# Routing tokens as two parts: one part's expert results scattered by token, the other's stored by tile and gathered at the end

## The chip, the cores and the metric

The kernel runs on one core of a Trainium2 chip, in one launch. The metric is the device time of that core in microseconds. Before the change it is 378.88 us, the median of 9 runs (375.48 to 384.29). The profile shows one execution of its own, which took 381.39 us; its span from the first to the last instruction is 379.7 us.

## The reference

Input x is 2 x 2048 tokens of 128 floats. Two blocks follow, each with a layer norm ahead of it and a residual around it:

```
x = x + attn(layernorm(x))    # a state-space layer: long convolution, gelu, a gated unit, a projection
x = x + ffn(layernorm(x))     # a mixture of experts
```

The second block is what matters here. Each of the 4096 tokens gets 14 gates (softmax of x @ router_w), keeps its top two and divides them by their sum. Expert e computes `silu(rmsnorm(x) * rms_w[e] @ w1[e]) @ w2[e]` with weights 128 x 256 and 256 x 128. The token's output is the gate-weighted sum of its two experts, plus two shared experts that every token passes through.

## The kernel before

Everything is float32. **The state-space layer** comes first and is left alone by the change.

**The routing stage** works on 32 chunks of 128 tokens, in five units u0 to u4 with chunks 0-3, 4-11, 12-19, 20-27 and 28-31 (class Unit, L657). A unit runs the gated unit and the output projection, adds to X, takes the layer-norm scales (`scales`, L720: some fourteen short VectorE operations), writes the normalised rows on ScalarE (`rows`, L735, into the tile `pl`), transposes them on TensorE, gets logits, picks two experts per token (`choose`, L777), counts tokens per expert (`count`) and turns counts into a slot number for each token and choice (`slots`, L826). `scatter` (L851) then issues two indirect DMAs per chunk on GpSimd (POOL). Each takes 128 rows of 130 floats (the row, its gate, and the number of the result row it belongs to) to their slots in the DRAM buffer `xs_rows`, where each expert has a region of its own. There are 64 such scatters.

**Shared experts** (class Shared, L946): eight blocks s0 to s7 of 512 tokens. Six of them stand in the hand-written list STEPS, between the units' steps; s6 and s7 come at the end (LATE = 2).

**The table** (`table`, L861): once all counts are known, about twenty short VectorE operations and a matmul give, for each tile of 128 slots, its expert and its first row.

**The tiles**: 77 tiles, a bound that holds for any counts. Per tile SP copies the expert's first weights into `wg` (L905, 12 tiles ahead), a DMA gathers 128 rows into `xg` (L911, 8 tiles ahead, on ScalarE's queue, the first even ones on SP's), TensorE transposes them (3 ahead), multiplies by `wg` (2 ahead), ScalarE applies silu (`hs`), and `outer` (L929) multiplies by the second weights, scales by the gate on VectorE (`yo`) and issues an indirect DMA on POOL that scatters 128 result rows by token into the DRAM buffer `res` (L940). Row numbers and experts are values in registers; every fourth tile ScalarE, SP and TensorE each load four of them (L1041). `xg` has 15 buffers and `yo` 10; the scatter reads its row numbers out of `xg`, so an `xg` buffer is free only when the scatter has landed.

**The end**: eight loads bring `res` back (L1003), s6 and s7 are computed, and VectorE adds the two results per token and X and stores (`finish`, L1006).

**Order.** From the routing stage on, VectorE, ScalarE and TensorE go through the wrapper Ordered (L643), which keeps their compute operations in the order in which they are written; the profile puts them all on L651. DMAs, register loads and everything on POOL are placed by the scheduler. Each engine then works through its own list from top to bottom, and a DMA issued from an engine's queue is an entry of that list.

Of the kernel before, what the change touches and what calls it, by code (L numbers as in the profile page):

```python
# [11 lines left out]
I32 = mybir.dt.int32  # L12
# [15 lines left out]
NTILE = (2 * NTOK + NE * (SLOTS - 1)) // SLOTS  # L28
ROW = P + 2
CAP = SLOTS + NTOK  # L30
# [19 lines left out]
u0.gate.0 u0.tanh.0 u0.value.0 u1.gate.0 u0.biased.0 u1.gate.1 u0.gated.0 u1.tanh.1  # L50
u1.value.1 u1.tanh.0 u0.project.0 u1.biased.1 u1.value.0 u0.add.0 u2.gate.1 u1.biased.0
u2.gate.0 u1.gated.1 u1.gated.0 u2.value.0 u2.tanh.0 u0.scales u1.project.0 u2.biased.0
u2.tanh.1 u1.project.1 u2.value.1 u1.add.0 u0.rows.0 u3.gate.0 u0.turn.0 u0.copies.0
u1.add.1 u0.turned.0 u2.biased.1 u0.logits.0 u1.scales u3.value.0 u2.gated.0 u1.rows.0
u0.unscale u2.project.0 u0.choose u1.rows.1 u1.turn.0 u1.copies.1 u2.add.0 u0.count u0.exps
u1.turned.0 u0.slots u1.turn.1 scale u1.logits.0 u1.turned.1 u1.copies.0 scale u1.logits.1
u1.unscale u0.scatter scale u2.gated.1 scale s0.first.0 scale u1.choose scale u2.project.1
s0.silu.0 scale u2.add.1 u1.count u1.exps s0.second.0 scale u1.slots scale scale u3.tanh.0
scale s0.first.1 scale u3.biased.0 u2.scales u1.scatter s0.silu.1 s0.second.1 u3.gated.0
u2.rows.0 s0.first.2 u2.rows.1 u2.turn.0 s0.first.3 s0.silu.2 u2.unscale s0.silu.3  # L60
s0.second.2 u2.turned.0 u2.turn.1 u2.logits.0 u2.turned.1 scale u2.logits.1 u2.copies.0
u3.project.0 u2.copies.1 u2.choose u3.gate.1 u4.gate.0 u3.tanh.1 u3.value.1 u4.tanh.0
u3.biased.1 u3.add.0 u2.count u4.value.0 u2.exps s0.second.3 u3.gated.1 u4.biased.0 u2.slots
s1.first.0 s1.first.1 s1.silu.0 u3.project.1 s1.silu.1 s1.second.0 u3.add.1 u2.scatter
s1.second.1 s1.first.2 s0.add u3.scales s1.silu.2 s1.second.2 u4.gated.0 u3.rows.0
s1.first.3 u3.rows.1 u3.turn.0 u4.project.0 u3.turned.0 u3.turn.1 u3.unscale u4.add.0
u3.turned.1 u3.logits.0 s1.silu.3 u3.logits.1 u3.copies.1 u3.copies.0 s1.second.3 u3.choose
s2.first.0 s2.silu.0 u3.count u3.exps s2.first.1 u3.slots s2.silu.1 s2.first.2 s2.first.3
u4.scales s2.second.0 u3.scatter s2.silu.3 s2.silu.2 s2.second.1 s1.add s2.second.2
u4.rows.0 s2.second.3 u4.copies.0 u4.turn.0 s2.add s3.first.0 u4.turned.0 u4.unscale  # L70
u4.logits.0 s3.silu.0 s3.first.1 u4.choose s3.silu.1 s3.second.0 s3.second.1 u4.exps
u4.count s3.first.2 u4.slots s3.silu.2 s3.first.3 s3.second.2 s3.silu.3 s3.second.3 s3.add
s4.first.0 s4.first.1 s4.silu.0 s4.first.2 s4.silu.1 s4.second.0 s4.silu.2 u4.scatter
s4.first.3 s4.second.1 s4.silu.3 scale s4.second.2 scale scale s4.second.3 s4.add s5.first.0
s5.first.1 s5.silu.0 s5.silu.1 s5.second.0 s5.second.1 s5.first.2 s5.silu.2 s5.first.3
s5.second.2 s5.silu.3 s5.second.3 s5.add
# [17 lines left out]
def s4d_glu_moe_kernel(  # L94
# [499 lines left out]
    pls = ctx.enter_context(tc.tile_pool(name="pls", bufs=3))  # L594
    xgp = ctx.enter_context(tc.tile_pool(name="xgp", bufs=15))
    yop = ctx.enter_context(tc.tile_pool(name="yop", bufs=10))
# [5 lines left out]

    xs_rows = nc.dram_tensor("xs_rows", (NE * CAP, ROW), F32).ap()
    xs_part = dram_disjoint_views(xs_rows, 2 * NT + 1)
    res = nc.dram_tensor("res", (2 * NTOK, P), F32).ap()
    res_part = dram_disjoint_views(res, NTILE)

# [467 lines left out]
    for _ in ends:  # L1077
        pass
# [49 lines left out]
```

## Time and profile before

| stage of the profiled execution | us from the span's start |
|---|---|
| state-space layer | 0 to 124 |
| routing up to the first scatter | 124 to 153.6 |
| scatters into xs_rows, 64 | 153.6 to 235.0 |
| table, first loads of weights and rows | 235 to 250 |
| 77 tiles on TensorE (first and last product `pz`) | 250.2 to 352.2 |
| last result scatter on POOL ends | 357.2 |
| loads of res, last sums, stores | 358.6 to 379.7 |

| engine | busy, us (share of the span) |
|---|---|
| TensorE (PE) | 270.7 (71%) |
| VectorE (DVE) | 231.3 (61%) |
| ScalarE (ACT) | 170.6 (45%) |
| GpSimd (POOL) | 148.6 (39%) |

The execution took 381.39 us, its span is 379.7 us, and the mean granted TensorE clock 0.873. The shares are averages over stages with different limits, so each stage is to be read by itself. In rows of the trace the first number is the start in us, the second the time in us, then engine, line, operation, what is written and read, and in brackets the engine's idle time before it and what ended that.

### The profile page before, as it was taken

To read this page: it belongs to the slowest core of one execution; us is meant where nothing else is said; L and a number is where in the kernel's file an instruction comes from. 1 tells how busy PE (TensorE), PEld (TensorE's weight loads), DVE (VectorE), ACT (ScalarE), POOL (GpSimd) and SP (SyncE) were. 2 spreads that over 40 slices of the span, in tenths; PEclk is the share of its full clock that TensorE was granted. 3 is DMA by queue.
4 is the path that set the end of the run, shared out by engine and by line. 5 is a ranking of instruction groups with operands and counts; after the bars stand their busy time and mean duration, and the time that the engine had idled before them with its cause. 6 is when DMAs were issued, how large, how long until landed. Compare 5 with 4: busy or idle time off the path is not lost.

```text
span 379.7 us, 8569 instructions
## 1 busy us (share of the span) xinstructions
PE 270.7 (71%) x2863; PEld 222.2 (59%) x2863; DVE 231.3 (61%) x718; ACT 170.6 (45%) x423; POOL 148.6 (39%) x230
## 2 busy tenths in 40 slices
PE   1900979748890997779798996087887778789940
PEld 1800659648790456546565774076787778779640
DVE  5789999999956298856857523133443444344074
ACT  3999869900233368967466542012322222323310
POOL 5300000000000200677777775036776776777400
PEclk9955599998995695789989699579999999999985
DMA  8100197953100790111111111267765656642098
GB/s 235 39 1 0 36 228 177 249 151 87 30 5 0 229 309 6 37 56 49 51 58 49 58 49 49 91 187 227 228 190 166 198 184 202 194 127 70 8 382 278
DMA packets 66894, 47.16 MB, mean 124 GB/s; under 512 B 7305, under 2 KB 64783, under 8 KB 66851
## 3 DMA queue, kind: packets, MB, share of 16 engines
q1 hardware_dynamic: 49714, 32.24, 28.6%
q0 software_dynamic: 4512, 8.47, 6.7%
q10 hardware_dynamic: 12624, 5.91, 6.1%
q8 instruction: 23, 0.38, 0.4%
q14 instruction: 21, 0.16, 0.1%
HBM read 24.49 MB, written 12.86 MB: 98 GB/s over the span
## 4 chain that ended last, share of the span: by engine, by line
DVE 39%; PE 31%; ACT 8%; issue 6%; DMA 5%; ACTq 5%; SPq 3%; POOL 1%; POOLq 0%; DVEq 0%
PE pz L651 11%; PE ph L651 8%; PE yps L558 4%; DVE t L329 3%; ACTq L1041 3%; DVE t L330 2%; ACTq L651 2%; PE pr L651 2%; DVE U L411 2%; ACT hs L651 2%; DMA xg<-xs_rows 2%; ACT junk L220 2%; DVE Y L568 2%; DVE sel L651 2%; ACT pl L651 2%
## 5 line engine op out<-in xcount | busy, mean ns | idle before, releaser
L940 POOL DMA_INDIRECT res<-yo,xg x77 | 75.7, 983 | 46.5 <-DMA xg<-xs_rows 17.0
L855 POOL DMA_INDIRECT xs_rows<-pl,si x64 | 62.0, 969 | 46.3 <-ACT WB L651 27.2
L651 ACT ACTIVATE hs<-ph 128x256 f32<-128x256 f32 x77 | 27.9, 382 | 90.4 <-PE ph L651 32.3
L651 DVE TENSOR_SCALAR yo<-pz,xg 128x128 f32<-128x128 f32 x77 | 27.0, 351 | 59.9 <-PE pz L651 57.6
L651 PE MATMUL pz<-WB,hs 128*128 x308 | 50.4, 286 | 17.0 <-ACT hs L651 16.6
L651 PEld LDWEIGHTS pz<-WB,hs 128*128 128x128 f32 x308 | 41.4, 193 | 21.6 <-ACT hs L651 20.5
L651 PE MATMUL ph<-xgt,wg 128*128 128x128 f32 x308 | 48.5, 281 | 0.2 <-DVE xgt L651 0.2
L651 PEld LDWEIGHTS ph<-xgt,wg 128*128 128x128 f32 x308 | 41.9, 197 | 0.6 <-DVE xgt L651 0.6
L613 POOL MEMSET blank<- 128x130 f32 x1 | 0.2, 207 | 97.5 <-DVE Y L568 97.5
L651 PEld LDWEIGHTS pz<-WB,hsh 128*128 128x128 f32 x192 | 25.5, 210 | 12.4 <-ACT hsh L651 9.5
L651 PE MATMUL pz<-WB,hsh 128*128 128x128 f32 x192 | 27.1, 298 | 4.9 <-ACT hsh L651 4.9
L651 DVE COPY xgt<-xgt 128x128 f32<-128x128 f32 x77 | 21.6, 282 | 10.9 <-PE xgt L651 10.8
L651 PE MATMUL xgt<-ident,xg 128*128 128x128 f32 x77 | 21.5, 282 | 9.1 <-DMA xg<-xs_rows 9.1
L651 PE MATMUL ph<-XRT,WB 128*128 128x512 f32 x48 | 27.8, 693 | 0.0
L651 ACT ACTIVATE hsh<-ph 128x512 f32<-128x512 f32 x24 | 14.0, 596 | 20.5 <-PE ph L651 20.5
L345 PE MATMUL kps<-PW,BC 128*8 128x128 f32 x128 | 6.5, 343 | 20.4 <-ACT junk L231 18.4
L472 PE MATMUL SP<-U,VT 128*32 128x32 f32 x512 | 14.2, 305 | 7.8 <-issue 5.3
L472 PEld LDWEIGHTS SP<-U,VT 128*32 128x32 f32 x512 | 13.5, 155 | 8.4 <-issue 5.7
L651 ACT ACTIVATE pl<-X,mr,rq_y 128x128 f32<-128x128 f32 x32 | 12.9, 482 | 12.0 <-DVE mr L651 12.0
L651 PE MATMUL pg<-Y,gluw 128*128 128x512 f32 x16 | 9.4, 706 | 10.8 <-DVE Y L568 10.8
L558 PE MATMUL yps<-PW,ST 32*32 32x128 f32 x512 | 15.2, 268 | 2.4 <-issue 1.6
L651 PEld LDWEIGHTS xgt<-ident,xg 128*128 128x128 f32 x77 | 11.1, 146 | 9.8 <-DMA xg<-xs_rows 9.8
(236 smaller groups left out, 549.9 us busy)
## 6 DMA issues: line engine op xcount, KB each, us to landing
wg<-WB SPq DMA_DIRECT2D x77, 128.0 KB
toep<-kp SPq DMA_DIRECT2D x24, 256.0 KB
xg<-xs_rows ACTq DMA_DIRECT2D x73, 65.0 KB
WB<-res SPq DMA_DIRECT2D x7, 512.0 KB
Y<-kp SPq DMA_DIRECT2D x8, 256.0 KB
WB<-in_w_dram SPq DMA_DIRECT2D x2, 896.0 KB
WB<-in_w_dram SPq DMA_DIRECT2D x4, 448.0 KB
out_dram<-WB SPq DMA_DIRECT2D x7, 256.0 KB
```

Of the source, the lines that this page charges most:

```text
L220: S.activation(junk, X[:, k, :], AF.Copy, accum_out=nm[:, k:k + 1])
L329: V.tensor_tensor(t1, low, bc(bc(Z[:, 0, k, qs], 1, 2), 3, m), ALU.mult)
L330: V.tensor_tensor(t2, low, bc(bc(Z[:, 1, k, qs], 1, 2), 3, m), ALU.mult)
L345: T.matmul(kps[a * NM:a * NM + 8, :], lhsT=BC[:, c, q, :], rhs=PW[:, c, q, 0:P], start=(i == 0 and c == 0), stop=False, skip_group_check=True,
L411: V.scalar_tensor_tensor(U[:, c, :], pu[:, k, :], rsr[:, c:c + 1], inb, ALU.mult, ALU.add)
L472: T.matmul(sp[j * NM:(j + 1) * NM, c, q - x * HQ, :], lhsT=VT[:, c, q, j * NM:(j + 1) * NM], rhs=U[:, :, 4 * q + j], start=True, stop=True,)
L558: T.matmul(ysum[g][js, u, :], lhsT=ST[js, c, q, :], rhs=PW[js, c, q, 1:P + 1], start=False, stop=(c == 1), skip_group_check=True,)
L568: V.transpose(Y.rearrange("p k t -> p t k"), YC)
L651: return tc.keep_in_program_order(getattr(self.engine, name)(*args, **kwargs))
L855: G.indirect_dma_start(out=xs_part[2 * (k0 + k) + a], out_offset=bass.IndirectOffsetOnAxis(ap=si[:, a, k:k + 1], axis=0), in_=pl[:, a, k, ...
L940: G.indirect_dma_start(out=res_part[t], out_offset=bass.IndirectOffsetOnAxis(ap=xg[:, P + 1:P + 2].bitcast(I32), axis=0), in_=yo, in_offse ...
L1041: return nc.values_load_multi_w_load_instructions(where[0:1, i, t:min(t + GRP, NTILE)], engines=engines, min_val=0, max_val=most, skip_run ...
```

## The change

Tokens go in two parts, chunks 0-19 (u0, u1, u2) and chunks 20-31 (u3, u4), each with an `xs_rows`, a count and a table of its own. Part 0 has 53 tiles and part 1 has 37, 90 in all. Part 0's results are scattered by token into `res` as before. Part 1's are stored tile by tile into a new DRAM buffer `ys` by a plain DMA on SP's queue, and at the end 24 indirect DMAs on POOL (`picked`, L1044 of the changed kernel) gather each token's two rows from `ys`. The tile loop runs over part 0 and then part 1.

STEPS is a new order. Shared experts s0 to s3 stand in it, and s4 to s7 come at the end. `table.0` follows `u2.slots`, and `table.1` follows `u4.slots`. The source emits u4's eight scatters one per tile in the loop (HELD = 8). `pl` has 4 buffers for 3, `yo` 14 for 10. The last block of `finish` is done in two halves.

```diff
-NTILE = (2 * NTOK + NE * (SLOTS - 1)) // SLOTS
-CAP = SLOTS + NTOK
+FROM, TO = (0, 20), (20, NT)
+NTILE = [NE + (2 * (b - a) * P - NE) // SLOTS for a, b in zip(FROM, TO)]
+CAP = [SLOTS + (b - a) * P for a, b in zip(FROM, TO)]
...
+u2.copies.1 u2.logits.0 u2.turned.1 u3.gate.0 u2.logits.1 u3.tanh.0 u3.value.0 u2.choose
+s1.first.0 u3.biased.0 u4.gate.0 s1.silu.0 u3.value.1 u3.gated.0 u2.count u2.exps
+u3.project.0 u3.biased.1 u2.slots table.0 u2.copies.0 s1.second.0 scale scale scale scale
+u4.value.0 scale u3.gated.1 u3.add.0 u4.tanh.0 u3.project.1 u4.biased.0 s1.first.1 u3.add.1
+s1.silu.1 s1.first.2 s1.second.1 u3.scales s1.silu.2 scale s1.first.3 scale s1.second.2
+s1.silu.3 u2.scatter u3.rows.0 s1.second.3 s1.add s2.first.0 u3.rows.1 s2.first.1 u3.unscale
+u3.copies.1 u3.turn.1 u4.gated.0 u3.turn.0 u3.turned.1 s2.first.2 u3.turned.0 u4.project.0
...
+s3.second.3 u4.slots table.1 s3.add u4.scatter
...
-    pls = ctx.enter_context(tc.tile_pool(name="pls", bufs=3))
+    pls = ctx.enter_context(tc.tile_pool(name="pls", bufs=4))
...
-    yop = ctx.enter_context(tc.tile_pool(name="yop", bufs=10))
+    yop = ctx.enter_context(tc.tile_pool(name="yop", bufs=14))
...
         def scatter(self):
+            self.left = [(k, a) for k in range(self.K) for a in range(2)]
+            while len(self.left) > (HELD if self is steps["u4"] else 0):
+                self.scatter_one()
+
+        def scatter_one(self):
             k0, pl, si = self.k0, self.pl, self.si
-            for k in range(self.K):
-                for a in range(2):
-                    G.indirect_dma_start(
...
+            k, a = self.left.pop(0)
+            G.indirect_dma_start(
+                out=xs_part[2 * (k0 + k) + a + self.p],
...
         yo = yop.tile([P, P], F32, name="yo")
         V.tensor_scalar(yo, pz, xg[:, P:P + 1], None, ALU.mult)
+        if p:
+            Q.dma_start(out=ys[t * SLOTS:(t + 1) * SLOTS, :], in_=yo)
+            return
...
+    def picked(j, rd):
+        for i in range(TB):
+            c = j * TB + i - TO[0]
+            for a in range(2):
+                G.indirect_dma_start(
+                    out=rd[:, i, a * P:(a + 1) * P], out_offset=None, in_=ys,
+                    in_offset=bass.IndirectOffsetOnAxis(
+                        ap=own[:, a, c:c + 1], axis=0
+                    ),
+                )
...
+            outer(p, t, xgs.pop(i), experts.pop(i), hss.pop(i))
+            wgs.pop(i)
+            if steps["u4"].left:
+                steps["u4"].scatter_one()
...
+    first_late, second_part = 4, TO[0] // TB
     rds = [summands(j) for j in range(NB)]
+    for j in range(second_part):
+        fetched(j, rds[j])
+    for j in range(second_part, NB):
+        picked(j, rds[j])
+    for j in range(first_late):
+        finish(j, rds[j], Q)
+    for j in range(first_late, NB):
+        for _ in steps[f"s{j}"].whole():
+            pass
+        finish(j, rds[j], Q, TB if j < NB - 1 else 2)
```

## The prediction, made before the result was known

> **What bounds the kernel now.** I read the page's slices first, then the rows of POOL, then ScalarE's waits, then the end.
>
> ```profile
> ## 2 busy tenths in 40 slices
> PE   1900979748890997779798996087887778789940
> ...
> POOL 5300000000000200677777775036776776777400
> ...
> L940 POOL DMA_INDIRECT res<-yo,xg x77 | 75.7, 983 | 46.5 <-DMA xg<-xs_rows 17.0
> L855 POOL DMA_INDIRECT xs_rows<-pl,si x64 | 62.0, 969 | 46.3 <-ACT WB L651 27.2
> ```
>
> A slice is 9.5 us. POOL reads 6 or 7 tenths from slice 16 on, with one hole at slices 24 and 25. That is no slack, as its rows in order of time show:
>
> ```profile
> 153.57 1.19 POOL L855 DMA_INDIRECT xs_rows<-pl,si  x1 [26.92 <-ACT WB L651]
> 155.07 0.96 POOL L855 DMA_INDIRECT xs_rows<-pl,si  x1 [0.30 <-issue]
> ...
> 204.94 0.96 POOL L855 DMA_INDIRECT xs_rows<-pl,si  x1 [0.31 <-issue]
> ...
> 234.00 0.95 POOL L855 DMA_INDIRECT xs_rows<-pl,si  x1 [0.30 <-issue]
> 251.93 0.99 POOL L940 DMA_INDIRECT res<-yo,xg  x1 [16.97 <-DMA xg<-xs_rows]
> ```
>
> Each indirect DMA holds POOL 0.96 us and is followed by 0.30 us of issue: 64 scatters from 153.57 to 234.95 are 1.27 us each, back to back. The result scatters stand 1.29 us apart where they do not wait (0.98 + 0.30). So POOL bounds 153 to 235, idles 17 us over table and first loads, and runs close behind TensorE in the tile loop. There the pace has another source:
>
> ```profile
> 299.44 0.38 ACT L651 ACTIVATE hs<-ph 128x256 f32<-128x256 f32 x1 [0.62 <-DVE xgt L651]
> 299.66 2.26 ACTq L651 DMA_DIRECT2D xg<-xs_rows  x2
> 302.03 0.66 ACT L651 ACTIVATE hs<-ph 128x256 f32<-128x256 f32 x2 [2.21 <-DMA xg<-xs_rows]
> ```
>
> ScalarE takes its list in order: a gather, the register load of every fourth tile (L1041, 1.25 us), a gather, and only then `hs`. Between 297.82 and 340.33 the rows of `yo` come in groups of four, eight groups, 5.31 us each or 1.33 us a tile; at the end, with no register loads left, 1.0 us. The waits between 255 and 345 us say the same:
>
> ```profile
> ACT hs L651 <- DMA xg<-xs_rows: 27.2, 13, 2.3
> ```
>
> A gather that has to wait holds ScalarE's compute behind it. The end is loads, adds and stores; the last store is issued at 374.52 and the span ends 5.2 us later:
>
> ```profile
> 358.58 5.84 SPq L1003 DMA_DIRECT2D WB<-res  x7
> ...
> 374.52 0.38 SPq L1011 DMA_DIRECT2D out_dram<-rd  x1
> ```
>
> **The change, part by part.** POOL issues 141 indirect DMAs before and after (64 + 77; 64 + 53 + 24), so its total is the same. What counts is where it waits. The built lists of the changed kernel show two things that its source does not. On POOL all 64 scatters still stand ahead of the first result scatter: u4's eight are not held. And on ScalarE the first three row gathers of part 0 stand between the silu of s1 and `u3.rows`, with waits for all 40 scatters of u0 to u2.
>
> *Up to u2.* VectorE does one more 0.69 us operation ahead of `u0.slots`: first scatter at 154.3. `u2.scales` (2.8 us) moves ahead of `u1.slots`, ready at 163.3 before: POOL waits about 1.7 us. 40 x 1.265 + 1.7 = 52.3 takes POOL to 206.6. The last result scatter took 2.09 us from issue to landing, so the 40th lands at 205.3 + 2.1 = 207.4.
>
> *ScalarE's wait.* Its work ahead of the gathers is what it did before `u3.rows` (188.53) plus two weight scalings of 0.5 us; `table.0` (4.3 us on VectorE) delays `u3.scales`, to about 193 to 196. So it waits from there to 207.4, with `u3.rows`, transposes, logits and choice of u3 queued behind, and TensorE behind the silu of s1. The table and the scalings hide below that wait; without it they cost up to 4.3 us. Then two gathers, a register load and a gather: 2.26 + 0.5; silu 0.6: rows at 210.8.
>
> *From rows to slots*, before:
>
> ```profile
> 188.53 3.19 ACT L651 ACTIVATE pl<-X,mr,rq_y 128x128 f32<-128x128 f32 x8 [2.36 <-DVE mr L651]
> ...
> 202.89 0.17 DVE L651 COPY pl<-goal 128x16 int32<-128x16 int32 x1
> ```
>
> That is 14.5 us. Now three 128x512 products (0.9 each) stand ahead of the logits and `u4.scales` (2.8) ahead of `u3.slots`: 14.5 + 5.4 = 19.9, u3 ready at 230.7. Bounds: 14.5 if they fit into gaps; 24, if TensorE comes back at half rate (four products 1.06 us at 247 to 250, 0.61 later) and its register loads fall in too. POOL idles 24.1 us. This is the new cost.
>
> *Then POOL alone.* u4 is ready long before its turn (13.3 us from its rows). 24 x 1.265 = 30.4: 261.1. 53 result scatters x 1.29 = 68.4: 329.5. TensorE starts tiles at about 250, since u4's choice, `table.1` and the new row sums come first, and gets nine tiles ahead: the gather of tile 15 needs the buffer of result 0, and `hs` of tile 9 stands behind it. So from 261 on tiles follow POOL at 1.29, not 1.33.
>
> *What POOL no longer limits.* Tile 69's gather waits for result 52, which lands at 330.3; `hs` of tile 63 stands behind it: 0.8, 331.1. The 27 tiles 63 to 89: five groups of 5.32 and seven of 1.0 are 33.6: 364.7. SP's 37 stores to `ys`: per four tiles 4 x 0.63 for `wg`, 4 x 0.5, and 1.05 for registers, 5.6 us against 5.32; the lead of 12 tiles hides it, 2 us if not. The first `wg` loads (12 x 0.63 + 3 x 1.05 = 10.7) follow 207 and end before 250.
>
> *The end.* On SP the first load of `res` waits for the last product and stands ahead of the last store of `ys`. That load took 4.1 us before; the store lands about 1 us later, at 369.8 (2.3, the least landing of a row gather, to 6 after the product). Then 24 gathers. No row shows an indirect gather: between a plain load's 0.63 on SP and the longest scatter, 1.28 + 0.30 = 1.58; I take 1.29, the nearest kind. 31.0: 400.8, landed 401.6. Two half-size adds 0.8, store and close 5.2: 407.6. s4 to s7 on TensorE (7.5 each, 350.7 to 358.3 for s6) end at 394.7, under the gathers; without them they would be 30 us. More `pl` and `yo` buffers: nothing by themselves.
>
> The span goes from 379.7 to 407.6, +27.9. The profiled execution, 381.39, stands 2.5 above the median; on the median 378.88 this is 406.8.
>
> A rule speaks for the early gathers: the Trainium skill, "DMA: Bandwidth & Descriptors", Rules for kernel authors, has DMAs issued early and their semaphores awaited late; by it the wait would cost nothing and the sum be 383.5. The same page, Anatomy of one DMA, says that a DMA's own semaphore wait happens on the issuing sequencer, before dispatch; by that it is 407.6. The 27.2 us above is the second.
>
> **The rivals.** *ScalarE is not held* (the other side): the gathers' wait ends by the time it reaches them. POOL then runs on from 206.6, and all after it moves by 24.1: 383.5, +3.8 in the span, 382.7 on the median, just within 1%. From u3's first scatter at 206.6 on, each us of delay is a us of the end. For it: POOL had u3 in time before. Against: no list order lets 40 x 1.265 end before 205. *Cheap gathers*: at 0.63 the end loses 24 x 0.66 = 15.8: 391.0. Against: every indirect row is 0.95 or more. *Dear gathers or a long u3 chain*: +7.0 or +4.1: 411 to 418. *The change does not do what it says*: its tiles do not run beside sorting on POOL at all. That much I take as given; it would spare nothing more.
>
> **How the numbers follow.** The forecast, 398 to 411 with the bounds of the u3 chain (-5.4, +4.1) and of the store (-2.5, +1), 0.72; cheap gathers 0.09; dear ones or a long chain 0.10; ScalarE not held 0.09, of which faster 0.02, within 1% 0.05, slower 0.02. So faster 0.02, same 0.05, slower 0.93; 1% is about what a measurement here can tell. The range of 8 in 10 reaches from 391 (cheap gathers) to 417.
>
> **What would show it.** A hole in POOL of 20 us or more after its 40th scatter; ScalarE idle before `u3.rows`, released by the DMA of `xg`; the first result scatter at about 261, right after the 64th scatter; 24 rows of 1.29 us at the end with TensorE done before them. Wrong would be: a POOL without that hole, gathers far from 1.29, or tiles past 63 at another pace than 1.33.

## The result and the profile after

The changed kernel takes 421.22 us, the median of 20 runs (418.39 to 423.08), against 380.21 for the kernel before (62 runs): a ratio of 1.1114 [1.1089, 1.114]. The forecast was 406.8. The sign and the main cause (row gathers that hold ScalarE) were right; the size was 14.4 us short, and the time lies 4.2 above the range, which reached to 417. The profiled execution took 424.3 us, its span is 422.6, and the mean granted clock 0.846.

| step (us from the span's start) | forecast | measured |
|---|---|---|
| first scatter | 154.3 | 153.40 |
| POOL waits for u1 | 1.7 | 5.12 |
| 40th scatter ends | 206.6 | 208.94 |
| gathers of part 0 released, u3's rows start | 207.4, 210.8 | 210.79, 213.74 |
| u3's rows to its first scatter | 19.9 | 20.1 |
| POOL idle after the 40th scatter | 24.1 | 24.87 |
| first result scatter | 261.1 | 264.16 |
| `hs` of tile 63 | 331.1 | **343.86** |
| from there to the last `yo`, tiles 63 to 89 | 33.6 | 34.0 |
| last `yo` to first final gather | 5.1 | 5.9 |
| 24 final gathers | 31.0 | 31.0 |
| after them to the end | 6.8 | 7.9 |

These are the changed kernel's slices of PE and POOL, and its three groups of indirect DMAs (busy time and mean ns, then the idle time before them). A slice is 10.6 us; counted from 0, POOL reads 0 in slices 20 and 21, the pause after the 40th scatter, and in 32 to 35, between the last result scatter and the first gather (49.6 us).

```profile
PE   3605997688729798754078666588779888899930
...
POOL 4300000000020034777600677777777300005771
...
L876 POOL DMA_INDIRECT xs_rows<-pl,si x64 | 61.9, 967 | 75.0 <-issue 40.7
...
L973 POOL DMA_INDIRECT res<-yo,xg x53 | 52.2, 985 | 18.1 <-issue 8.2
L1044 POOL DMA_INDIRECT WB<-ys,own x16 | 16.1, 1007 | 54.1 <-DMA WB<-res 49.6
```

POOL's rows in order of time show the hole after the 40th scatter, the 64th scatter with the first result right behind it, the last two result scatters and the ends of the row of gathers:

```profile
207.98 0.96 POOL L876 DMA_INDIRECT xs_rows<-pl,si  x1 [0.31 <-issue]
233.81 0.96 POOL L876 DMA_INDIRECT xs_rows<-pl,si  x1 [24.87 <-issue]
...
262.89 0.96 POOL L876 DMA_INDIRECT xs_rows<-pl,si  x1 [0.30 <-DMA xs_rows<-pl,si]
264.16 1.00 POOL L973 DMA_INDIRECT res<-yo,xg  x1 [0.30 <-DMA xs_rows<-pl,si]
...
331.94 0.98 POOL L973 DMA_INDIRECT res<-yo,xg  x1 [0.30 <-issue]
333.23 0.98 POOL L973 DMA_INDIRECT res<-yo,xg  x1 [0.30 <-issue]
383.76 1.15 POOL L1044 DMA_INDIRECT WB<-ys,own  x1 [49.55 <-DMA WB<-res]
...
413.79 0.95 POOL L1044 DMA_INDIRECT rd<-ys,own  x1 [0.30 <-issue]
```

ScalarE's rows say why u3 was late. It stood idle from 193.73 on; the gathers at the head of its list were issued at 210.79, and the silu and u3's rows came after them:

```profile
192.84 0.90 ACT L657 ACTIVATE WB<-WB,rms 128x256 f32<-128x256 f32 x2
210.79 2.41 ACTq L657 DMA_DIRECT2D xg<-xs_rows  x3
213.24 0.60 ACT L657 ACTIVATE hsh<-ph 128x512 f32<-128x512 f32 x1 [19.51 <-DMA xg<-xs_rows]
213.74 1.64 ACT L657 ACTIVATE pl<-X,mr,rq_y 128x128 f32<-128x128 f32 x4
```

The next lines are SP's at the end. The loads of `res` and the last store of `ys` follow the last product, as forecast; seven stores lie between 384.06 and 418.53, and the last two follow the last gather. TensorE's last products, those of the shared experts, end at 405.0, 9.8 us before the last gather leaves POOL, so it is the gathers that the end waits for:

```profile
377.92 0.40 SPq L1038 DMA_DIRECT2D WB<-res  x1
378.41 0.58 SPq L971 DMA_DIRECT2D ys<-yo  x1
379.04 2.86 SPq L1038 DMA_DIRECT2D WB<-res  x4
384.06 34.47 SPq L1058 DMA_DIRECT2D out_dram<-WB  x7
419.21 0.92 SPq L1058 DMA_DIRECT2D out_dram<-rd  x2
```

One thing has to be known for the numbers below: the kernel before took 379.7 to 382.1 us beside four of the experiments, as here, but 448.9 to 452.8 beside the fourteen others, which ran on other chips, so each experiment is read only against runs of its own kind; and the ratios leave out executions over 1.5% above the fastest of their kernel, so they can differ a little from those of the medians.

### The profile page after: what moved, and what is told of

It reads as the page before. It is cut to its first block, busy times and chain, and to the rows that moved or that the text cites. A ratio compares the mean times of both kernels' runs of the same rounds, so it can differ in the third digit from the quotient of the medians.

```text
span 422.6 us, 9094 instructions
## 1 busy us (share of the span) xinstructions
PE 290.4 (69%) x2982; PEld 242.1 (57%) x2982; DVE 241.1 (57%) x770; ACT 174.3 (41%) x436; POOL 149.9 (35%) x244
## 4 chain that ended last, share of the span: by engine, by line
PE 14%; issue 12%; POOL 9%; DMA 7%; ACTq 5%; ACT 2%; DVE 1%; POOLq 0%; SPq 0%; DVEq 0%
PE pz L657 8%; PE ph L657 5%; POOL xs_rows L876 4%; POOL WB L1044 4%; DMA xs_rows<-pl,si 3%; ACTq L1090 3%; ACTq L657 2%; ACT hs L657 2%; DMA res<-yo,xg 1%; POOL rd L1044 1%; PE xgt L657 1%; DMA WB<-res 1%; DMA rd<-ys,own 1%; DMA xg<-xs_rows 0%; DVE xgt L657 0%
## 5 line engine op out<-in xcount | busy, mean ns | idle before, releaser
L657 PE MATMUL pz<-WB,hs 128*128 x360 | 61.5, 293 | 25.9 <-ACT hs L657 23.8
L657 PEld LDWEIGHTS pz<-WB,hs 128*128 128x128 f32 x360 | 50.4, 199 | 31.6 <-ACT hs L657 28.0
L657 PE MATMUL ph<-xgt,wg 128*128 128x128 f32 x360 | 57.6, 284 | 2.1 <-DVE xgt L657 2.1
L973 POOL DMA_INDIRECT res<-yo,xg x53 | 52.2, 985 | 18.1 <-issue 8.2
L657 PEld LDWEIGHTS ph<-xgt,wg 128*128 128x128 f32 x360 | 50.0, 201 | 2.5 <-DVE xgt L657 2.5
L1044 POOL DMA_INDIRECT WB<-ys,own x16 | 16.1, 1007 | 54.1 <-DMA WB<-res 49.6
L657 PE MATMUL pz<-WB,hsh 128*128 128x128 f32 x128 | 20.2, 316 | 20.0 <-ACT hsh L657 20.0
L657 PEld LDWEIGHTS pz<-WB,hsh 128*128 128x128 f32 x128 | 18.9, 227 | 24.8 <-ACT hsh L657 22.9
L657 ACT ACTIVATE hsh<-ph 128x512 f32<-128x512 f32 x16 | 9.5, 599 | 27.6 <-DMA xg<-xs_rows 19.5
L657 PE MATMUL ph<-XRT,WB 128*128 128x512 f32 x32 | 19.7, 711 | 0.0
L345 PE MATMUL kps<-PW,BC 128*8 128x128 f32 x128 | 6.5, 343 | 19.0 <-ACT junk L231 18.4
L472 PE MATMUL SP<-U,VT 128*32 128x32 f32 x512 | 13.6, 297 | 6.8 <-issue 4.3
L558 PEld LDWEIGHTS yps<-PW,ST 32*32 32x32 f32 x512 | 15.6, 112 | 3.9 <-issue 3.0
```

The source lines that it names most:

```text
L345: T.matmul(kps[a * NM:a * NM + 8, :], lhsT=BC[:, c, q, :], rhs=PW[:, c, q, 0:P], start=(i == 0 and c == 0), stop=False, skip_group_check=True,
L472: T.matmul(sp[j * NM:(j + 1) * NM, c, q - x * HQ, :], lhsT=VT[:, c, q, j * NM:(j + 1) * NM], rhs=U[:, :, 4 * q + j], start=True, stop=True,)
L558: T.matmul(ysum[g][js, u, :], lhsT=ST[js, c, q, :], rhs=PW[js, c, q, 1:P + 1], start=False, stop=(c == 1), skip_group_check=True,)
L657: return tc.keep_in_program_order(getattr(self.engine, name)(*args, **kwargs))
L973: G.indirect_dma_start(out=res_part[t], out_offset=bass.IndirectOffsetOnAxis(ap=xg[:, P + 1:P + 2].bitcast(I32), axis=0), in_=yo, in_offse ...
L1044: G.indirect_dma_start(out=rd[:, i, a * P:(a + 1) * P], out_offset=None, in_=ys, in_offset=bass.IndirectOffsetOnAxis(ap=own[:, a, c:c + 1] ...
```

## The experiments

Theory H (the prediction's): the gathers of part 0 in ScalarE's list hold u3, POOL pauses for it, and every us of that pause is a us of the end; the final gathers are a bare tail. Rivals: the pause is covered by something else and moving the gathers gives little; the tail or the 13 more tiles are the real price. Open beside these is whether POOL's result scatters set the tiles' pace, as the prediction has it. The four experiments beside which the kernel before took 380 come first.

### pinned_loads_d: ScalarE's register loads stay where the source has them

With the loads kept at their place in the list, the row gathers that need their values fall behind u3's and u4's steps too. `keep_in_program_order` keeps an instruction at its place in the source's order.

```diff
-        return enumerate(
-            nc.values_load_multi_w_load_instructions(
...
-            )[1]
+        loads, vals = nc.values_load_multi_w_load_instructions(
...
         )
+        for ld in loads:
+            if ld.ins.engine == ACT_:
+                tc.keep_in_program_order(ld)
+        return enumerate(vals)
```

> ScalarE's register loads in the order of the source, all else as in the changed kernel; once more, for the last runs were on a chip on which the kernel before takes 382 again. Theory 'held', now with u2_split's times: u3's rows at 193 to 194 instead of 213.7, u3's first scatter at 212 to 213 instead of 233.8, so a hole of 3 to 4 us behind the 40th scatter at 209 (24.9 in the changed kernel). POOL goes on without a break to the 64th, 22 us earlier, and the first result scatter stands at 242 to 243. Tiles start at 220 to 224, stop at tile 9 until result 0 has landed (about 12 us longer than before), and are 20 to 22 us earlier from there on: 399 to 402. Rival 'the tiles bind from their start' (no loss at tile 9): 30 earlier, 390 to 393. Rival 'not on the path': 417 to 421.

Measured: 401.62 us (396.25 to 402.94) beside 379.7, ratio 1.0535 [1.0392, 1.0678]; that is 19.6 below the changed kernel's median. The span is 400.3, 22.3 shorter. POOL's rows around the 40th scatter and around the first result, and ScalarE's row with u3's rows:

```profile
210.50 0.96 POOL L876 DMA_INDIRECT xs_rows<-pl,si  x1 [0.30 <-issue]
215.95 0.96 POOL L876 DMA_INDIRECT xs_rows<-pl,si  x1 [4.48 <-ACT hsh L657]
...
245.01 0.95 POOL L876 DMA_INDIRECT xs_rows<-pl,si  x1 [0.30 <-DMA xs_rows<-pl,si]
246.27 1.00 POOL L973 DMA_INDIRECT res<-yo,xg  x1 [0.30 <-DMA xs_rows<-pl,si]
...
197.06 3.19 ACT L657 ACTIVATE pl<-X,mr,rq_y 128x128 f32<-128x128 f32 x8 [0.62 <-DVE mr L657]
```

ScalarE's wait for the gathers of part 0 fell from 19.5 to 1.8 us and u3's rows went from 213.74 to 197.06. POOL's hole fell from 24.87 to 4.48, 20.4 us, and the span by 22.3. The two are not quite the same: POOL's first result came 17.9 earlier (the first scatter stood 2.1 later), the tiles from 9 to 63 took 5.6 less (ScalarE's order in the tile stage changed as well), and 1.3 were lost behind them. Still, no cover lies under the pause, and H holds for it. It is half of the loss, not all: 20.6 us of span remain over the kernel before. Here the tiles do run beside the sorting (first `yo` 232.85, last scatter 245.96), and they again stop at tile 9, for 8.6 us, until the first result has landed.

### u2_split: part 0's last scatters behind u3's

Register loads as above; POOL's scatters kept in the order of the source, with eight of u2's put behind u3's and u4's eight among the tiles.

```diff
-            while len(self.left) > (HELD if self is steps["u4"] else 0):
+            while len(self.left) > (HELD if self is steps["u4"] or self is steps["u2"] else 0):
                 self.scatter_one()
+            while self is steps["u3"] and steps["u2"].left:
+                steps["u2"].scatter_one()
...
-            G.indirect_dma_start(
+            tc.keep_in_program_order(G.indirect_dma_start(
```

> Loads in order as before, and POOL's scatters in the order of the source: 8 of u2's 16 behind u3's, u4's 8 one by one between the first result scatters (which is what the source of the changed kernel says and its build does not do). POOL's first stretch is 32 scatters and ends at about 199 instead of 209. In all runs of this series engines with ready inputs stood still until POOL's stretch had drained. Theory 'the stop lasts as long as POOL issues': ScalarE goes on at 199 to 203 instead of 209 to 214, u3's first scatter 9 to 10 us earlier, at 221 to 230. Theory 'the stop has its own length': ScalarE goes on at 209 to 214 as before, u3 at 231 to 240. The 8 scatters behind u3's give the time back on POOL; u4's held ones let the first result scatter start 10 us earlier relative to the 56th: time 452 to 465.

Measured: 418.45 us (415.14 to 422.63), ratio 1.0968 [1.089, 1.1046], span 413.4. ScalarE now waits later and longer, at the head of the tile stage:

```profile
244.26 2.43 ACTq L657 DMA_DIRECT2D xg<-xs_rows  x3
246.72 1.28 ACT L657 ACT_TABLE_LOAD   x1 [29.69 <-DMA xg<-xs_rows]
```

Part 0's rows cannot be gathered before its last scatter, and that scatter now stands behind u3's. The tiles start at 249.89, almost where the changed kernel's do (251.03). But with u4's eight scatters among them there is no stop at tile 9: in the two profiled executions tile 52 comes 8.6 us earlier (322.31 for 330.93, of which 1.1 lies in the start), the last tile 9.1, and the span ends 9.2 earlier. That would make the stop a second loss beside the hole. But the profiled execution is the fastest of the four here (415.14) and the slowest of all there (424.3); on the medians the run gains only 2.8 us, and it changes more than the stop. So the price of the stop is not shown. The expectation was worked out for the chips on which the kernel before takes 450; the stop of ScalarE that it asks about is not there in this run.

### gather_both: part 0 stored and gathered as well

All 90 tiles store to `ys`, and 64 gathers stand at the end; there are no result scatters.

```diff
-        if p:
-            Q.dma_start(out=ys[t * SLOTS:(t + 1) * SLOTS, :], in_=yo)
-            return
-        G.indirect_dma_start(
-            out=res_part[t],
...
+        t += p * NTILE[0]
+        Q.dma_start(out=ys[t * SLOTS:(t + 1) * SLOTS, :], in_=yo)
...
-    for j in range(second_part):
-        fetched(j, rds[j])
-    for j in range(second_part, NB):
+    for j in range(NB):
         picked(j, rds[j])
```

> Part 0's results are stored tile by tile too, so no result scatter is left in the tile loop, and all 64 gathers stand at the end; 90 tiles, two tables and the order of the steps as in the changed kernel. What it tells is the pace of part 0's tiles with POOL silent. In the changed kernel part 0 ran at 1.45 us a tile when first profiled and at 1.70 in the repeat, part 1 (no POOL) at 1.27 and 1.3 in both. Theory 'own pace, made slower by the result scatters': 1.27 to 1.35 from the first tile on, no stop at tile 9, last product 115 to 121 us behind the first. Theory of the prediction, 'the result scatters' 1.29 pace part 0 and the tiles alone run at 1.33': the same pace of 1.33 but for the stop at tile 9. Rival 'part 0 is slow for another reason' (stores on SP, transposes): 1.45 or more. The end: 64 gathers of 1.28 are 82 us where 24 were 31, so 462 - 30 + 51 = 478 to 490.

Measured: 467.01 us (465.33 to 467.46), ratio 1.2204 [1.2145, 1.2263], span 463.6. The first and last of the 64 gathers:

```profile
377.14 0.98 POOL L1035 DMA_INDIRECT WB<-ys,own  x1 [114.68 <-issue]
...
457.24 0.94 POOL L1035 DMA_INDIRECT rd<-ys,own  x1 [0.30 <-issue]
```

80.1 us for 63 intervals, 1.27 each: a gather at the end costs its whole 1.27 us, and 40 more of them cost 51. The expected 478 to 490 was worked out from 462, the changed kernel's time on the other chips; here the run is 45.8 above the changed kernel's 421.2. That is less than 51, and one thing that is spared is the stop at tile 9, gone with the result scatters (tile 8 at 259.33, tile 9 at 261.42). With no indirect DMA on POOL, tiles 9 to 52 still take 1.51 us each (1.45 in the changed kernel), and ScalarE waits 20.9 us for row gathers there. So to take the result scatters away does not quicken the tiles. As 53 stores on SP took their place, the run does not show what sets the pace.

### no_tail: no hold, no gathers

Register loads kept, POOL in the source's order, part 1 scattered by token like part 0, and s4 and s5 ahead of the tiles.

```diff
-        if p:
-            Q.dma_start(out=ys[t * SLOTS:(t + 1) * SLOTS, :], in_=yo)
-            return
         G.indirect_dma_start(
-            out=res_part[t],
+            out=res_part[p * NTILE[0] + t],
...
-s3.second.3 u4.slots table.1 s3.add u4.scatter
+s3.second.3 u4.slots table.1 s3.add u4.scatter s4.first.0 s4.first.1 s4.silu.0 s4.first.2 s4.silu.1 s4.second.0 s4.silu.2 s4.first.3 s4.second.1
...
-    first_late, second_part = 4, TO[0] // TB
+    first_late, second_part = 6, TO[0] // TB
```

> Four edits: ScalarE's register loads and POOL's scatters in the order of the source (u4's 8 between the first results), part 1's results scattered by token as well (no gathers at the end, 90 result scatters), and s4 and s5 ahead of the tile loop as in the kernel before. It asks what is left of the change's idea without its two costs. POOL issues 64 + 90 = 154 indirect DMAs where the kernel before issues 141, so 13 x 1.29 = 16.8 us more, and has no more of the 17 us in which it idled over table and first loads. Result 0 at about 236; then 98 indirect DMAs of 1.29 on POOL (362) or 89 tiles of 1.40 (361); 22.5 us of loads, sums and stores as in the kernel before: 381 to 388, within 2% of the kernel before's 380 to 382. Theory 'a draw': that. Rival 'the idea wins once its costs are gone': 375 or less. Rival 'tiles and scatters slow each other down': 392 or more.

Measured: 391.79 us (389.66 to 392.62), ratio 1.0332 [1.0255, 1.0409], span 390.9: the nearest that these four come, and still slower. POOL pauses before its first result, and then works without a pause to its last:

```profile
230.13 0.96 POOL L878 DMA_INDIRECT xs_rows<-pl,si  x1 [0.30 <-issue]
243.15 0.99 POOL L972 DMA_INDIRECT res<-yo,xg  x1 [12.06 <-DVE xgt L659]
...
368.03 0.98 POOL L972 DMA_INDIRECT res<-yo,xg  x1 [0.30 <-issue]
```

POOL's account: from its first scatter to its last result it takes 214.6 us (154.40 to 369.01), before 203.6, so 11.0 more. Thirteen more DMAs are 12.6 of busy time (150.3 for 137.7) and 13 x 0.30: 16.5. Idle time beyond the 0.30 after each DMA is 18.4 (span less busy less 153 x 0.30), before 23.9: 5.5 saved. The end after it is nearly the same (21.9 and 22.5). Sorting beside the tiles wins POOL's idle time at most, and the rounding up of a second part to whole tiles costs more than it won here.

### after_again, before_again: the two kernels on other chips

The changed kernel and the kernel before, unedited, where the kernel before takes 450 us.

> The changed kernel itself, unaltered, beside the kernel before. On the chips of the eight runs so far the kernel before took 452 us, not 380; this run says what the changed kernel takes under the same conditions, and so what those eight are to be compared with. If the chips are as in the first measurement: 380 and 421, ratio 1.11. If they are as in the eight runs: the ratio of 1.11 carried over gives 502, and then the loads in order (469) are worth 33 and the scatter of both parts (457) 45. If the slowness hits waits between engines alone (VectorE's dependent steps of the table stood 1.3 to 2.5 us apart there, 0.2 to 0.3 here), the changed kernel, with two tables, loses more than the kernel before.

> The kernel before, unaltered, with a profile under the conditions of the experiments (where it takes 450 us, 70 more than when it was first profiled). Theory 'engines stand still while POOL issues indirect DMAs': it shows nothing new up to the first scatter (153 us), then waits of ScalarE or VectorE of 10 to 30 us whose inputs are ready, and 77 result scatters at over 1.5 us each instead of 1.37; the stages without indirect DMAs (0 to 153, and the last 22) take what they took. Rival 'the chip is slower all through': every stage 18% longer.

Measured: after 462.05 (459.24 to 463.93), ratio 1.0286 [1.0202, 1.037]; before 450.06 in its one run, span 448.4. In the kernel before the stages without indirect DMAs are as long as ever: the first scatter stands at 151.04, and the end behind the last result takes 22.5 us, as it did. What grew lies beside or between indirect DMAs: 77 result scatters come 1.72 us apart for 1.37. In the changed kernel 24 gathers take 30.7 (31.0), but the end behind them 15.4 for 7.9, and ScalarE stops at an operation that waits for no gather ("remote" is a release whose source the profile does not tell):

```profile
184.24 0.67 ACT L657 ACTIVATE th<-pg,glubh 128x512 f32<-128x512 f32 x1
213.58 0.69 ACT L657 ACTIVATE av<-pa,glub 128x512 f32<-128x512 f32 x1 [28.66 <-remote]
```

It stands still until 4.5 us after the 40th scatter's start (209.03). The product that it reads was late itself and ended at 202.55, so that for 11 of the 28.66 us it had its input. The gathers then hold ScalarE for 2.36 us, not for 19.5: u3 is late without them. Why the engines stop is not shown.

### pinned_loads, pinned_loads_b, pinned_loads_c: the first edit again, there

> ScalarE's register loads are kept in the order of the source, so the row gathers of part 0 stand behind u4's rows and no longer ahead of u3's. Everything else is as in the changed kernel. Theory 'held' (ScalarE's early gathers make POOL's hole of 24.9 us and the whole of it reaches the end): u3's rows start at about 193 instead of 213.7, the hole shrinks to 5 us or less, and everything behind it moves by 20 to 24 us: 397 to 401. Theory 'own pace' adds to it: with the result scatters and the tiles moving together, the tiles also have POOL's scatters of u3 and u4 still ahead of the first result scatter, so the stall of 8 us at tile 9 stays within 3 us of what it was; same total. Rival 'late slots' (u3's slots are late for another reason: four 128x512 products and u4.scales stand in the chain anyway): hole 15 us or more, 410 or above. Rival 'not on the path' (the end is set by the 90 tiles, which start at 251 whatever POOL does): within 3 us of 421.

> The same kernel as pinned_loads, again, because on that run's chip the kernel before took 452 us instead of 380 and one wait of 30 us, which no instruction of the kernel ends, lay on the path. ScalarE's register loads in the order of the source, so part 0's row gathers stand behind u4's rows. Theory 'held': u3's rows at about 193, POOL's hole 5 us or less, all behind it 20 to 24 us earlier: 397 to 401. Rival 'late slots': hole 15 us or more, 410 or above. Rival 'not on the path': within 3 us of 421.

> Once more ScalarE's register loads in the order of the source. In the runs so far every kernel, this one too, has a hole of 24 to 31 us in POOL behind the 40th scatter, which ends when the scatters have drained. If the chip is as in the first measurement (before: 380), theory 'held' says u3's rows at about 193, a hole of 5 us or less and 397 to 401; rival 'late slots' a hole of 15 us or more and 410 or above. If it is as in the later runs (before: 450), the hole is again 24 to 31 us whether or not the gathers stand ahead of u3's rows, and the time is within 2% of the changed kernel's 462.

Measured: 470.53, 469.42 and 472.19 us, ratios 1.037 [1.0289, 1.045], 1.0363 [1.0236, 1.049] and 1.0479 [1.0405, 1.0552]. Taken alone, this refutes H. But the profile of the first shows that the edit could not act: no gather stands ahead of ScalarE's stop, and it lasts as long. (In the second the stop is shorter, 14.27 and then 9.25 us, and POOL's hole 23.59.)

```profile
211.75 0.69 ACT L657 ACTIVATE av<-pa,glub 128x512 f32<-128x512 f32 x1 [31.98 <-remote]
```

In the first POOL's hole is 29.39 us and ends with u3 at 238.93. With that stop gone, in pinned_loads_d, the same kernel gains 19.6.

### code_shift and pinned_code_shift: is the stop at a place in ScalarE's list?

32 tiny copies early in ScalarE's list; the second with the register loads kept.

```diff
+EXTRA = 32
...
+        spare = big.tile([P, 1], F32, name="spare")
+        for k in range(EXTRA):
+            tc.keep_in_program_order(S.copy(spare, nb[:, 0:1]))
```

> The changed kernel with 32 copies of one column put into ScalarE's list at 60 to 75 us, where ScalarE idles. They write a spare tile that nothing reads; the rest of the list is unaltered and stands 32 places further back. In five kernels run so far ScalarE stood for 24 to 33 us ahead of its 316th instruction (av of u4) until the 40 scatters had drained, and for 27 to 31 us ahead of the 375th or 380th; in one of them the inputs of the 316th were ready 30 us before. Theory 'code supply' (the engine waits for its next stretch of instructions, which comes late while POOL issues indirect DMAs): the place moves with the count, to the instruction that was the 284th to 288th (u2's rows or silu, at 158 us) and to the 344th to 348th (at 223 us); av of u4 waits 10 us or less. Time 440 to 470. Rival 'the instruction itself waits' (an input that the profile does not show): the stop stays at av of u4, 24 to 33 us, and the time is within 1% of 462.

> The same 32 copies, with ScalarE's register loads in the order of the source. Theory 'code supply' and theory 'held' together: av of u4 does not stop, no gather holds u3's rows, and POOL's hole behind the 40th scatter is 10 us or less: 15 to 25 us less than code_shift, in which the gathers still hold ScalarE until the 40th scatter has landed (hole 24 to 31). If the gathers cost nothing here: both the same within 1%. If the stop stays at av of u4: 469 as without the copies.

Measured: 469.53, ratio 1.0361 [1.0285, 1.0436], and 462.84, 1.018 [1.0098, 1.0262]. The stop (32.3 and 33.7 us) stayed at the same instruction, u4's `av`, though its place in the list moved by the copies. A cause tied to the place, such as a late supply of code, falls. The trace of after_again fits: from 198.2 to 215.0 its instruction queues carry no packet, while the stop ends at 213.58.

### scatter_both and scatter_both_b: part 1 by token as well

The edit of no_tail to `outer` and the end, and nothing else.

> Part 1's results are scattered by token into res like part 0's: 37 result scatters more on POOL, no stores of ys and no gathers at the end; eight plain loads of res. The two tables, 90 tiles, the order of the steps and ScalarE's early gathers are as in the changed kernel. Theory 'gathers are a serial tail': the last result scatter ends some 3 us behind the last product (381), loads and sums of res took 22.5 us behind it in the kernel before: 404. Theory 'shared experts next': s4 to s7 end 28 us behind the last product at 378 (405 to 406), then two adds, store and close of 7 us: 411 to 414. Rival 'gathers cost nothing' (they lie beside TensorE's work): 419 to 423.

> The same kernel as scatter_both, again, for the same reason. No gathers at the end and no stores of ys; 37 result scatters more. Theory 'gathers are a serial tail': 404. Theory 'shared experts next' (s4 to s7 on TensorE, 28 us behind the last product at 378, set the end): 411 to 414. Rival 'gathers cost nothing': 419 to 423.

Measured: 459.25, ratio 1.0144 [1.0092, 1.0196], and 456.95, 1.0073 [1.0032, 1.0115]. With scatters, the tiles from 52 to the last take 1.70 and 1.75 us each, for 1.29 in after_again, and from the start of the last result scatter to the end it is 30.5 and 31.2 us. Against after_again's 1.0286 that is 1.4 to 2.1% less: there the tail of gathers costs more than the faster tiles bring.

### loads_of_8 and loads_of_8_b: eight values per register load

```diff
-AHEAD, LEAD, GRP, TWO = 12, 8, 4, 8
+AHEAD, LEAD, GRP, TWO = 12, 8, 8, 8
```

> Register loads bring eight tiles' values at a time instead of four (all three engines). A four-tile group took 5.0 to 5.6 us against 1.0 us a tile without loads. Theory 'own pace' (from tile 9 on the tiles run at their own pace, 1.43 us in part 0, and POOL only just waits for them): half of the 1.3 us a group goes, 0.15 us a tile over the tiles that POOL lets go faster; POOL's 1.29 then bounds part 0 (tile 61 about 4.5 us behind the 53rd scatter at 332, so 5 us earlier) and the 28 tiles behind it win 20 x 0.16 = 3: -7 to -10, 411 to 414. Theory of the prediction, 'POOL paces part 0': only the tiles behind it win, -3 to -4.5: 417 to 418. Rival 'the load costs by the value': no change, 420 to 422.

> The same kernel as loads_of_8, again, for the same reason. Register loads of eight tiles' values at a time. Theory 'own pace' (from tile 9 on the tiles run at their own pace of 1.43 us in part 0, POOL only just waits for them): 411 to 414. Theory of the prediction, 'POOL paces part 0': 417 to 418. Rival 'the load costs by the value': 420 to 422.

Measured: 471.01 beside 452.13, and 469.28, ratio 1.035 [1.0264, 1.0435]. From tile 52 to the last the pace went from 1.29 in after_again to 1.44 and 1.39. ScalarE's loads (ns: least, median, most) of four values in after_again, and of eight in loads_of_8_b:

```profile
L1090 ACTq TENSOR_LOAD <-where x24: 291/1077/1257, 214.0 to 400.8; - x24
```

```profile
L1090 ACTq TENSOR_LOAD <-where x12: 1279/2046/2106, 213.4 to 399.6; - x12
```

The load costs by the value, not by the instruction: half as many loads save nothing and stop ScalarE for twice as long.

### pinned_split28 and pinned_split28_b: part 1 of four chunks

```diff
-FROM, TO = (0, 20), (20, NT)
+FROM, TO = (0, 28), (28, NT)
...
-u3.project.0 u3.biased.1 u2.slots table.0 u2.copies.0 s1.second.0 scale scale scale scale
+u3.project.0 u3.biased.1 u2.slots u2.copies.0 s1.second.0 scale scale scale scale
```

`table.0` goes behind `u3.slots`, and the register loads are kept.

> As with the loads in order, and the cut between the parts lies at chunk 28 instead of 20 (69 tiles and 21 instead of 53 and 37; table.0 behind u3.slots). The gathers at the end are 8 instead of 24, all other counts are the same: 90 tiles, 141 indirect DMAs. If the gathers at the end cost 1.29 us each and are the path, 16 fewer are -20.7 us. But s4 to s7 on TensorE (7.0 to 7.5 us each behind the last product, 28 to 30 us) were hidden under them: with only 5.9 + 10.3 us of cover they end 12 to 14 us later than the gathers and set the end, so theory 'shared experts next' says -9 to -11 against the kernel with the loads in order, and +3 to +4 for part 0's first rows, which now wait for 56 scatters: 388 to 394 if that one runs at 398. Rival 'gathers alone': -20, 378.

> The same kernel as pinned_split28, again, for the same reason. Loads in order, cut at chunk 28: 8 gathers at the end for 24. Theory 'shared experts next': -9 to -11 for the gathers, +3 to +4 for the later first rows, against pinned_loads_b: 388 to 394 if that one runs at 398. Rival 'gathers alone': -20, 378.

Measured: 454.55, ratio 0.9935 [0.9837, 1.0033], and 453.79, 0.9842 [0.9749, 0.9934]. Against the same kernel cut at chunk 20 (470.53 and 469.42) that is some 16 us less, between the two expectations. Only eight gathers are left, and in the second run the end from the first of them is 27.5 us (418.94 to 446.5) for 46.0 in after_again. It is the one version about level with the kernel before: its medians are 2.4 and 1.0 us above that one's, its ratios a little below 1, so that no gain is shown. And it was tried only where the kernel before takes 450.

### best_guess: all of it

Register loads kept and of eight values, 28 and four chunks, s4 and s5 ahead of the tiles.

> Four edits together: ScalarE's register loads in the order of the source, the cut at chunk 28 (8 gathers), s4 and s5 back ahead of the tile loop (s6 and s7 at the end), register loads of eight tiles. On a chip as in the first measurement: no hole in POOL over 6 us, 64 scatters end at 238 to 241, 69 result scatters to 329, tile 69's product at 322, 21 tiles of 1.16 to 1.33 to 346 to 350, then 5.9 + 10.3 + 7.9: 370 to 374, against 380 of the kernel before. If a register load costs by the value: 376 to 380. If s6 and s7 set the end: 14 to 15 us of TensorE, 2 us of add and 5.2 of close behind the last product: 372. Rival 'still 90 tiles' (the 13 tiles more cost what the gathers spare): 385 or above. On a chip where the kernel before takes 452: 0.95 to 0.99 of it.

Measured: 458.70, ratio 1.0232 [1.0165, 1.0299]. ScalarE's stop at u4's `av` is there with 30.00 us though its inputs were done at 179.2, and the loads of eight cost what they cost above. It is slower than pinned_split28 alone.

## Why the prediction was right in kind and wrong in size

**The hold: right.** ScalarE waited 19.5 us for part 0's gathers, POOL 24.87 for u3, and in pinned_loads_d, where the gathers have left ScalarE's list there, 20.4 of that pause and 22.3 of the span are gone.

**POOL up to its first result: 3.1 short.** The first scatter came 0.9 earlier than forecast, the wait for u1 was 3.4 longer, the hole 0.8 longer (u3 began 2.9 later, but POOL's 40th scatter ended 2.3 later too): 264.16 for 261.1, right after the 64th scatter, as it should be. The wait for u1 is 5.12 in pinned_loads_d too, but 2.6 in u2_split and gather_both; what decides it is not shown.

**The step that failed: "from 261 on tiles follow POOL at 1.29", and with it "`hs` of tile 63 stands behind it: 0.8, 331.1".** Tile 63's `hs` stands at 343.86, the second of the two in this row:

```profile
343.57 0.66 ACT L657 ACTIVATE hs<-ph 128x256 f32<-128x256 f32 x2 [1.86 <-DMA xg<-xs_rows]
```

These 12.8 us are most of the miss of 15.0 in the span. The forecast had the tiles nine to eleven ahead of POOL all the way, held back only by it, so that 27 were left at 331.1, when POOL's last result had landed. In fact they ran slower than POOL, 1.42 us a tile, and lost that lead: at 331.1 the next `hs` was that of tile 54, and 36 were left. Nine tiles at 1.33 are 12.0. Where the lead went:

- 3.1 us are POOL's first result, as above. The stop at tile 9 behind it is as forecast: `hs` waits until that result has landed and comes 2.8 us after its issue (264.16); the forecast's landing of 2.1 and its 0.8 are 2.9.

```profile
266.97 0.38 ACT L657 ACTIVATE hs<-ph 128x256 f32<-128x256 f32 x1 [7.95 <-DMA res<-yo,xg]
```

- From `hs` of tile 9 to that of tile 63 it took 76.9 us, 1.42 a tile, where the forecast had 67.1. Of these 9.8 us, 2.6 are a slip in its sum, which gives 54 tiles only 52 steps of 1.29. With 15 buffers the gather of tile 67, not 69, needs the buffer of result 52, as that of tile 15 needs that of result 0, and it is `hs` of tile 61 that stands behind it; 54 steps are 69.7.
- Another 2.1 are the pace. Groups of four from tile 13 to 33 took 5.2 to 5.6 us, about the 1.33 of the kernel before, and slower than POOL's 1.29. At 1.33, 54 tiles are 71.8. From tile 20 on no gather waits for a result to land.
- The last 5.1 lie in two places (5.7 by the rows of `yo`): 8.0 us from tile 9 to 13 and 13.6 from 33 to 41, where the pace gives 5.3 and 10.6. In the first the tiles were still held by POOL: the gathers of tiles 16 to 19 are issued at 268.18, 269.14, 270.50 and 272.95, and by the trace's semaphores the last three wait for results 2, 3 and 4 to land; `hs` of tile 13 stands behind the last, at 275.48. In both places TensorE also ran below its full clock, after 6.86 us idle at 267 and 1.57 at 308. These rows are windows of the changed kernel (start, length, busy of PE, PEld, DVE, ACT, POOL, then the granted clock, DMA share, GB/s):

```profile
266.00:271.00 5.00, 3.59 (x17) 3.60 (x18) 0.96 (x4) 1.15 (x3) 3.78 (x5) 0.50 0.32 88
271.00:308.00 37.00, 29.20 (x237) 27.49 (x236) 14.39 (x53) 8.94 (x25) 28.18 (x29) 0.99 0.61 186
308.00:313.00 5.00, 3.90 (x19) 3.72 (x20) 1.10 (x4) 1.04 (x3) 3.94 (x4) 0.66 0.43 135
313.00:333.00 20.00, 16.93 (x136) 15.52 (x134) 8.23 (x30) 5.05 (x14) 13.79 (x14) 1.00 0.57 175
```

At the end of part 0 it is POOL that waits for tiles, not tiles for POOL:

```profile
329.35 0.99 POOL L973 DMA_INDIRECT res<-yo,xg  x1 [1.62 <-DVE yo L657]
```

gather_both fits this: without result scatters, though with more stores on SP, the pace is no better. In pinned_loads_d, where POOL issued its 53 results 1.29 apart without a wait, tiles 9 to 52 did follow it, at 1.31; why they keep up there is not shown. The two limits lie 0.04 us apart; the forecast took the lower one as the only one, while the wait for the slower was named in its first part. How much of the 5.1 the clock cost is not shown; no run took the idle gaps away by themselves.

**Behind tile 63: right.** 27 tiles 34.0 for 33.6, the store 5.9 for 5.1, 24 gathers 31.0 for 31.0, the end 7.9 for 6.8. 12.8 + 0.4 + 0.8 + 1.1 = 15.1, against 422.6 - 407.6 = 15.0.

**The rivals.** *ScalarE is not held* was priced at 383.5 as if nothing else were late; with the hold gone pinned_loads_d has a span of 400.3. The hold's price (24.1; 20.4 us of pause gone, 22.3 on the spans, 19.6 on the medians) was about right. Of the 16.8 that are left, 9.3 are POOL's first result, at 246.27 for 237.0 with pauses of 5.12 and 4.48 still there, and 4.2 the tiles from 9 to 63, with the forecast's slip among them. *Cheap gathers* and *dear gathers* fall: 0.95 + 0.30 at the median. *A long u3 chain* falls: 20.1. *That the change does not do what it says* holds for most of it: nine tiles ran before the last scatter, and then stopped for POOL.

**The rule on issuing early.** The Trainium skill, "DMA: Bandwidth & Descriptors", Rules for kernel authors, has DMAs issued early and awaited late; its section Anatomy of one DMA puts a DMA's own wait on the sequencer that issues it. The 19.51 us row and pinned_loads_d decide for the second.

## What to carry to other kernels

A DMA that must wait is an entry in its engine's list: look in the built list for what stands behind it, for the source does not show where a scheduler puts it. Where two engines pace a stage by nearly the same step (1.29 and 1.33 here), reckon the lead of the one over the other at the start and at the end of the stage, and count every stop as a loss of lead; what matters is how many tiles are left when the last release comes. Splitting work in two to fill an engine's idle time also rounds up twice: 13 more tiles at 1.28 us of POOL are all of the 17 us that it could have filled.

## What the runs showed of the hardware that was not expected

- On four chips both kernels were slower by different amounts: before 448.9 to 452.8 us for 380 on all four, changed 462 for 421 on the one where it ran unedited. In the kernel before, stages without indirect DMAs kept their length; beside POOL's scatters ScalarE stood still for up to 33.8 us (loads_of_8), in best_guess for 30.00 with its inputs ready. That the chips were others, and the hour too, is all that is known of the cause.
- A register load on ScalarE takes 1.08 us for four values and 2.05 for eight; SP's take 0.30 and 0.57, TensorE's 0.34 and 0.66 (medians of after_again and loads_of_8_b).
- An indirect gather of 128 rows holds POOL as a scatter does: 0.95 and 0.30 us of issue.
- Idle gaps of 1.57 and 0.46 us were followed by a clock that reads 0.66 over the 5 us from 308, and four products took 1.06 us there for 0.61. The length of the gap alone does not decide it: after 2.19 us in the same trace (before 275.91), and after 2.93 in gather_both (before 323.56), the clock stayed full: the windows 271 to 308 above and 320 to 333 there read 0.99 and 1.00. The Trainium skill, "TensorE: Matmul & The Clock Gate", Why this matters for your kernels, warns of gaps over about 3 us; here the clock fell without one that long, so the measurement decides.

```profile
308.64 0.49 PE L657 MATMUL pz<-WB,hs 128*128 x2 [1.57 <-ACT hs L657]
309.59 0.79 PE L657 MATMUL pz<-WB,hs 128*128 x2 [0.46 <-issue]
```
